# Moving a projection's first copy from ScalarE to VectorE in a fused attention kernel

## The chip, the cores and the metric

The kernel runs on one core of a Trainium2 chip. A core has TensorE (matrix products into PSUM, an on-chip memory of eight banks of 128 x 512 float32), VectorE (DVE), ScalarE (ACT), GpSimd (POOL), and DMA queues, here mostly those of SyncE (SP). The engines run side by side and wait for each other by semaphores; each works through its own instructions in order. The metric is the device time of one execution in microseconds (us), as the median of several runs.

## The reference

The input x is 8 batches of 512 rows of 512 numbers; cond is one row of 512 per batch. Attention with 16 heads of 32 is computed in float32:

```python
Q = x @ Wq.T + bq;  K = x @ Wk.T + bk;  V = x @ Wv.T + bv      # split into heads
cQ = Q + (cond @ Wq.T + bq);  cK = K + (cond @ Wk.T + bk)
scores = einsum('bhqd,bhkd->bhqk', cQ, cK) / sqrt(32)
out = x + merge_heads(softmax(scores) @ V)
```

## The kernel before

**Tiles.** Four heads fill the 128 partitions, so there are four head groups per batch and T = 32 of them in all; t counts them. For each t the scores are computed twice. One pass has queries on the partitions: `row_max` makes the scores of 128 queries for four heads (`row_scores`, L499), VectorE takes each row's maximum, negated (L490 for one bank, L508 for two at once), and `denominators` (L518) lets ScalarE compute exp(score - maximum) with a running sum; only the sum is kept. The other pass has keys on the partitions: `exponentials` puts the maxima into PSUM with four small bf16 products (L570), adds the scores (L573), and ScalarE writes their exponentials e (L584), which `weighted` multiplies by V (L589). The maxima get from one layout to the other by `split_max` (four small GpSimd operations that split each into three bf16 parts, L532 to L535) and `turn_max` (a transposing DMA, L544, in SP's queue).

**Projections.** Q, K and V of the next batch are made by a scheme of seven half-size products in place of eight (as Strassen's). `first_products` makes products 1, 6, half of 2, and 7; `other_products` makes 4, 5, the rest of 2, and 3. Each takes 14 matmuls of 256 columns (L403 for V, L406 for Q and K). In `first_products` the first product is copied out of its bank by ScalarE (L438, the result is called m1), and VectorE then makes three sums with it and the other products: c12 (L444), c1 (L445) and c22 (L429 for Q and K, L426 for V, by `plus`).

**The loop.** For t from 0 to 28 there are four stages, which are told apart below as the q, weighted, k and v stage. Each begins with `exponentials` for t (so with L570), then has `row_max` for a later quarter, and then either a projection with the denominators inside it (q, k and v stage) or the denominators and `weighted` for t - 1. At odd t the projections are `first_products`, at even t `other_products` (from t = 1 on). In the q stage a transpose of x on VectorE follows (`turn_x`, L323), in the k stage `split_max`, `turn_max` and the loads of the residual, which GpSimd adds to the bias (L173).

**Order and banks.** The order on TensorE, ScalarE, VectorE and GpSimd is the order of the program text; that of the DMAs in SP's queue is chosen by a planner. The banks are written out by hand: `TURNS` has a row of eight banks for each stage, the first four for `exponentials` and, when those have been read, for the projection, and the last four for the scores of `row_max`. Rows 4 to 7 are the four stages at odd t, rows 0 to 3 those at even t. A bank that a stage has filled last with scores is read by VectorE (maximum) and ScalarE (denominator) and is written again in the next stage:

```python
(6, 7, 4, 5, 0, 1, 2, 3),   # row 4, q stage at odd t: product 1 goes to bank 6, the scores to 0 to 3
(4, 5, 0, 1, 2, 3, 6, 7),   # row 5, weighted stage: its scores go to 2 and 3, and 6 and 7
(2, 5, 0, 1, 6, 7, 3, 4),   # row 6, k stage: product 1 in bank 2, scores in 6, 7, 3, 4
(6, 7, 0, 1, 2, 3, 4, 5),   # row 7, v stage: product 1 in bank 6, scores in 2 to 5
```

So in the weighted stage at odd t the first score takes the bank of the q stage's third denominator, the second that of the fourth, the third that of product 1 (read last by c22), the last that of c1. After the k stage the order is c22's bank, third, fourth, c1's; after the v stage third, fourth, c22's, c1's.

Of the kernel before, what the change touches and what calls it, by code (L numbers as in the profile page):

```python
# [12 lines left out]
ALU = mybir.AluOpType  # L13
AX = mybir.AxisListType
# [3 lines left out]
def kernel(  # L18
# [38 lines left out]
    nc = tc.nc  # L57
# [5 lines left out]
    HG = P // HD  # L63
# [4 lines left out]
    T = B * G  # L68
    HS = S // 2
# [42 lines left out]
    def banks(i, n=1):  # L112

        j = TURNS[turn[0]][i]
        if n == 1:
            return psum[:, j, :]
        k = TURNS[turn[0]][i + 1]
        return psum[:, j : k + 1 : k - j, :]
# [126 lines left out]
    for i in range(NS):  # L245
        r = slice(i * BL, (i + 1) * BL)
# [95 lines left out]
    def pair_of(t, n):  # L342

        if (n, t // 2) not in pairs:
            pairs[n, t // 2] = qkp.tile([P, 2, S], F32, tag=n, name=f"{n}T_{t // 2}")
        return pairs[n, t // 2]
# [50 lines left out]
    def product(n, b, u, i, pt, kcs=(0, 1)):  # L397

        for kc in kcs:
            w = block_of_w(n, i, u, kc)  # L400
            if n == "v":
                xb = block_of_x(b, i, kc, slice(u * P, (u + 1) * P))
                nc.tensor.matmul(pt, xb, w, start=(kc == kcs[0]), stop=(kc == kcs[-1]))  # L403
            else:
                xb = block_of_x(b, i, kc, slice(0, HS))
                nc.tensor.matmul(pt, w, xb, start=(kc == kcs[0]), stop=(kc == kcs[-1]))  # L406

    def twice(a):
        return a.unsqueeze(1).broadcast_to([P, 2, HS])

    def halves(a):
        return a.rearrange("p (h s) -> p h s", h=2)


    def parts_of(n, b, u):

        if n == "v":
            v = vs[b % 2]
            return v[:, u::2, :HS], v[:, u + 2, :HS], v[:, u::2, HS:], v[:, u + 2, HS:]
        o = pair_of(b * G + u * 2, n)  # L420
        return halves(o[:, 0, :]), o[:, 0, HS:], halves(o[:, 1, :]), o[:, 1, HS:]

    def plus(n, b, u, g, o, pt, rest):

        if n == "v":
            nc.vector.tensor_tensor(o, pt, rest, ALU.add)  # L426
        else:
            add = tok[:, "qk".index(n), u * 2 + g, b : b + 1]
            nc.vector.scalar_tensor_tensor(o, pt, add, rest, ALU.add, ALU.add)  # L429

    def first_products(n, b, u, dens, small, at, first=0):


        one_, two_ = banks(first), banks(at)
        c1, c12, c2, c22 = parts_of(n, b, u)
        m1 = c2[:, 0, :]
        product(n, b, u, 1, one_[:, :HS])
        nc.scalar.copy(m1, one_[:, :HS])  # L438
        dens()
        product(n, b, u, 6, two_[:, :HS])  # L440
        small()
        product(n, b, u, 2, two_[:, HS:], (0,))
        product(n, b, u, 7, one_[:, HS:])
        nc.vector.tensor_tensor(c12, two_[:, :HS], m1, ALU.add)  # L444
        nc.vector.tensor_tensor(c1[:, 0, :], two_[:, HS:], m1, ALU.add)  # L445
        plus(n, b, u, 1, c22, one_[:, HS:], c12)

    def other_products(n, b, u, dens, small, at):

        dens()  # L450
        one_, two_ = banks(at[0]), banks(at[1])
        product(n, b, u, 4, one_[:, :HS])
        product(n, b, u, 5, one_[:, HS:])
        small()
        product(n, b, u, 2, two_[:, :HS], (1,))
        product(n, b, u, 3, two_[:, HS:])
        c1, c12, c2, c22 = parts_of(n, b, u)
        nc.vector.tensor_tensor(c12, one_[:, HS:], c12, ALU.add)
        nc.vector.tensor_tensor(c2, halves(one_), twice(c22), ALU.add)
        plus(n, b, u, 0, c1, halves(two_), c1)  # L460
        if n != "v":
            for g in range(2):
                qkT[n, b * G + u * 2 + g] = pair_of(b * G + u * 2, n)[:, g, :]

    def project_pair(n, b, r, dens, small, at):

        if b >= B:
            dens()
            small()
        else:  # L470
            (first_products, other_products)[r % 2](n, b, r // 2, dens, small, at)


    nmax = {}
    sums = {}

    def open_max(t):
        if t not in nmax:
            nmax[t] = op.tile([P, NS, HG, 1], F32, tag="nmax", name=f"nmax_{t}", bufs=3)
            sums[t] = op.tile([P, NS, HG, 1], F32, tag="sums", name=f"sums_{t}", bufs=3)  # L480

    def row_max(t, qc):
        if t >= T:
            return
        open_max(t)
        for j in range(HG):
            row_scores(t, qc, j, banks(HG + j))
        if t < T - 2 or t * NS + qc == T * NS - 1:
            for j in range(2):
                nc.vector.tensor_reduce(  # L490
                    nmax[t][:, qc, j : j + 1, 0], banks(HG + j), AX.X, ALU.max, negate=True
                )
        else:
            row_max_of(t, qc, 0, banks(HG, 2))
        row_max_of(t, qc, 1, banks(HG + 2, 2))

    def row_scores(t, qc, j, pt):
        r = slice(j * HD, (j + 1) * HD)
        nc.tensor.matmul(  # L499
            pt,  # L500
            qkT["q", t][r, qc * P : (qc + 1) * P],
            qkT["k", t][r, :],
            start=True,
            stop=True,
        )

    def row_max_of(t, qc, pr, pt):
        nc.vector.tensor_reduce(  # L508
            nmax[t][:, qc, pr * 2 : pr * 2 + 2, 0], pt, AX.X, ALU.max, negate=True
        )  # L510

    def denominators(t, qc, prs=range(NP)):

        if t >= T - 2:
            return
        for j in [pr * 2 + i for pr in prs for i in range(2)]:
            dead = op.tile([P, S], F32, tag="dead", name=f"dead_{t}_{qc}_{j}")
            nc.scalar.activation(  # L518
                dead,
                banks(HG + j),  # L520
                AF.Exp,
                bias=nmax[t][:, qc, j, :],
                accum_out=sums[t][:, qc, j, :],
            )

    def split_max(t, on=nc.gpsimd):

        if t >= T:
            return
        m, sp = nmax[t], split[t % 2]  # L530
        rest = op.tile([P, NS, HG, 1], F32, tag="rest", name=f"rest_{t}")
        on.tensor_copy(sp[:, :, :, 0:1], m)  # L532
        on.tensor_tensor(rest, m, sp[:, :, :, 0:1], ALU.subtract)
        on.tensor_copy(sp[:, :, :, 1:2], rest)
        on.tensor_tensor(sp[:, :, :, 2:3], rest, sp[:, :, :, 1:2], ALU.subtract)  # L535
# [3 lines left out]
    def turn_max(t):  # L539

        if t >= T:
            return
        maxT[t] = op.tile([P, S], BF16, tag="maxT", name=f"maxT_{t}")
        nc.sync.dma_start_transpose(  # L544
            maxT[t].rearrange("p (c q) -> p c q", c=NS),
            split[t % 2].rearrange("p c h e -> p (c h e)"),
        )
# [258 lines left out]
    for t in range(T - 3):  # L806
        b, r = divmod(t, G)

        exponentials(t, 0)
        row_max(t + 1, 1)  # L810
        of = ((t - 1) // G + 1, (t - 1) % G)
        dens = lambda: denominators(t + 1, 1)
        if t:
            project_pair("q", *of, dens, nothing, 1 if r % 2 else (0, 3))
        else:
            first_products("v", 0, 0, dens, nothing, 1)
            turn_x(NC + 2)
            load_residual(1)
        turn_x(t + NC + 3)
        advance()  # L820

        exponentials(t, 1)
        row_max(t + 1, 2)
        dens = lambda: denominators(t + 1, 2)
        if t:
            dens()
            weighted(
                t - 1, banks(0), banks(1), lambda: combine_x(b + 1, r) if r < 2 else None
            )
        else:  # L830
            dens()
            other_products("v", 0, 0, nothing, nothing, (0, 2))
        advance()

        exponentials(t, 2)
        row_max(t + 1, 3)
        split_max(t + 1)
        turn_max(t + 1)
        dens = lambda: denominators(t + 1, 3)
        if t:  # L840
            project_pair("k", *of, dens, nothing, 1 if r % 2 else (0, 3))
        else:
            first_products("v", 0, 1, dens, nothing, 1)
            combine_x(1, 0)
        if t:
            load_residual(t + 1)
        advance()

        exponentials(t, 3)
        row_max(t + 2, 0)  # L850
        dens = lambda: denominators(t + 2, 0)

        project_pair("v", *of, dens, nothing, 1 if r % 2 else (0, 2))
        advance()


# [55 lines left out]
    t = T - 3  # L912
# [21 lines left out]
    t = T - 2  # L934
# [15 lines left out]
    pa, rest = banks(2), [1, 2, 3]  # L950
# [8 lines left out]
    t = T - 1  # L959
# [47 lines left out]
    b, g = divmod(t, G)  # L1007
# [55 lines left out]
```

## Time and the profile before

| | |
|---|---|
| median of 3 runs | 722.1 us (721.99 to 722.43) |
| profiled execution | 722.59 us, of which the span from the first to the last instruction is 720.8 |
| granted TensorE clock | 0.999 |
| TensorE, ScalarE, VectorE, GpSimd busy | 99%, 86%, 73%, 24% of the span |
| L438, ScalarE copy 128x256 | 46 instructions, 402 ns at the median for Q and K, 372 for V |
| L490, maximum of one bank | 240 instructions, 686 ns |
| L508, maximum of two banks | 130 instructions, 1214 ns |

A line of the timeline has start and length in us, the engine, the line of the program, what is written from what, and in brackets how long the engine had been idle and what it waited for; several like instructions can be merged (x4). PEld is TensorE's loading of weights, which runs ahead of the products. A line of the table by stretches has the stretch, its length, and for TensorE, weight loads, VectorE, ScalarE and GpSimd the busy time and the instructions, then the granted clock, the busy share of the DMA engines and GB/s. A line of the waits has total us, times, and the longest. Ends of matmuls are modelled, so a busy TensorE can still be a waiting one.

### The profile page before, as it was taken

To read this page: it belongs to the slowest core of one execution; us is meant where nothing else is said; L and a number is where in the kernel's file an instruction comes from. 1 tells how busy PE (TensorE), PEld (TensorE's weight loads), DVE (VectorE), ACT (ScalarE), POOL (GpSimd) and SP (SyncE) were. 2 spreads that over 40 slices of the span, in tenths; PEclk is the share of its full clock that TensorE was granted. 3 is DMA by queue.
4 is the path that set the end of the run, shared out by engine and by line. 5 is a ranking of instruction groups with operands and counts; after the bars stand their busy time and mean duration, and the time that the engine had idled before them with its cause. 6 is when DMAs were issued, how large, how long until landed. Compare 5 with 4: busy or idle time off the path is not lost.

```text
span 720.8 us, 14892 instructions
## 1 busy us (share of the span) xinstructions
PE 714.2 (99%) x5296; PEld 401.3 (56%) x5296; DVE 528.0 (73%) x834; ACT 617.3 (86%) x1539; POOL 176.3 (24%) x275
## 2 busy tenths in 40 slices
PE   9999999999999999999999999999999999999997
PEld 7566555565555566555565555565555565555532
DVE  4798777777768777677776877777767767767777
ACT  2589989999899998989999889998989989889674
POOL 3712221122221122221122221122221122221351
PEclk9999999999999999999999999999999999999999
DMA  6733321222322222321322321323201222211211
GB/s 177 110 60 62 53 41 30 49 44 46 53 35 36 50 41 49 53 41 28 51 41 49 52 40 27 53 37 52 38 16 23 38 38 38 37 21 19 37 32 29
DMA packets 223358, 32.91 MB, mean 46 GB/s; under 512 B 221610, under 2 KB 222122, under 8 KB 223284
## 3 DMA queue, kind: packets, MB, share of 16 engines
q1 hardware_dynamic: 221524, 30.92, 25.3%
q10 hardware_dynamic: 1760, 1.05, 0.5%
q8 instruction: 41, 0.67, 0.4%
q14 instruction: 33, 0.27, 0.1%
HBM read 19.75 MB, written 8.39 MB: 39 GB/s over the span
## 4 chain that ended last, share of the span: by engine, by line
PE 97%; DVE 2%; issue 1%; DMA 1%; DVEq 0%
PE psum L406 27%; PE psum L499 16%; PE psum L589 15%; PE psum L403 14%; PE psum L573 14%; PE psum L570 5%; PE psum L350 2%; DVE acc L863 1%; PE psum L889 1%; DMA w_q<-in_L_cond_Wq_dram 1%; PE psum L266 0%; DVE acc L861 0%; PE psum L311 0%; PE psum L667 0%; PE psum L599 0%
## 5 line engine op out<-in xcount | busy, mean ns | idle before, releaser
L518 ACT ACTIVATE dead<-psum,nmax 128x512 f32<-128x512 f32 x480 | 327.6, 702 | 5.1 <-DVE nmax L490 3.1
L584 ACT ACTIVATE e<-psum 128x512 f32<-128x512 f32 x488 | 252.0, 602 | 64.2 <-PE psum L573 63.9
L490 DVE TENSOR_REDUCE nmax<-psum 128x1 f32<-128x512 f32 x240 | 154.5, 686 | 143.1 <-PE psum L499 143.1
L508 DVE TENSOR_REDUCE nmax<-psum 128x2 f32<-128x1024 f32 x130 | 157.7, 1214 | 2.8 <-PE psum L499 2.7
L499 PE MATMUL psum<-kT,qT 32*128 32x512 f32 x1024 | 143.9, 605 | 0.0
L646 POOL TENSOR_TENSOR res<-res,recs 128x512 f32<-128x512 f32 x30 | 31.5, 1049 | 432.1 <-DVE res L645 432.1
L573 PE MATMUL psum<-qT,kT 32*128 32x512 f32 x976 | 125.5, 587 | 0.0
L589 PE MATMUL psum<-e,v 128*32 128x512 f32 x1024 | 121.2, 596 | 0.0
L518 ACT ACTIVATION_READ_ACCUMULATOR dead<-psum,nmax 128x1 f32 x480 | 105.2, 219 | 0.0
L499 PEld LDWEIGHTS psum<-kT,qT 32*128 32x128 f32 x1024 | 59.8, 183 | 58.1 <-ACT dead L518 26.4
L589 PEld LDWEIGHTS psum<-e,v 128*32 128x32 f32 x1024 | 26.6, 110 | 65.1 <-issue 37.6
L573 PEld LDWEIGHTS psum<-qT,kT 32*128 32x128 f32 x976 | 48.6, 185 | 2.2
L403 PE MATMUL psum<-wc_v,xc 128*128 128x256 f32 x192 | 49.3, 379 | 0.0
L570 PE MATMUL psum<-maxT,onesb 3*128 3x512 bf16 x488 | 48.1, 384 | 0.0
L406 PE MATMUL psum<-xc,wc_k 128*128 128x256 f32 x180 | 46.2, 379 | 0.0
L406 PE MATMUL psum<-xc,wc_q 128*128 128x256 f32 x180 | 46.2, 379 | 0.0
L570 PEld LDWEIGHTS <-onesb 3*128 3x128 bf16 x488 | 12.3, 90 | 57.2 <-issue 57.2
L173 POOL TENSOR_TENSOR xr<-xr,bvs 128x512 f32<-128x512 f32 x31 | 39.4, 1272 | 18.7 <-DMA x<-in_x_dram 12.0
L403 PEld LDWEIGHTS psum<-wc_v,xc 128*128 128x128 f32 x192 | 36.5, 190 | 5.0
L647 POOL TENSOR_TENSOR res<-res,xr 128x512 f32<-128x512 f32 x30 | 38.2, 1273 | 2.4
L403 PE MATMUL psum<-wT_v,xT 128*128 128x256 f32 x128 | 37.1, 392 | 0.0
L406 PEld LDWEIGHTS psum<-xc,wc_k 128*128 128x128 f32 x180 | 34.2, 190 | 4.7
(165 smaller groups left out, 791.2 us busy)
## 6 DMA issues: line engine op xcount, KB each, us to landing
xr<-in_x_dram SPq DMA_DIRECT2D x124, 64.0 KB, 2.4
out_dram<-res SPq DMA_DIRECT2D x122, 64.0 KB, 1.9
x<-in_x_dram SPq DMA_DIRECT2D x112, 64.0 KB, 2.4
w_q<-in_L_cond_Wq_dram SPq DMA_DIRECT2D x4, 256.0 KB, 4.4
w_v<-in_L_cond_Wv_dram SPq DMA_DIRECT2D x16, 64.0 KB, 2.4
w_k<-in_L_cond_Wk_dram SPq DMA_DIRECT2D x16, 48.0 KB, 2.3
x<-in_x_dram ACTq DMA_DIRECT2D x2, 256.0 KB, 3.9
x<-in_x_dram SPq DMA_DIRECT2D x2, 256.0 KB, 4.2
```

The costliest lines, as they stand in the source:

```text
L173: nc.gpsimd.tensor_tensor(xr[t], xr[t], bias, ALU.add)
L403: nc.tensor.matmul(pt, xb, w, start=(kc == kcs[0]), stop=(kc == kcs[-1]))
L406: nc.tensor.matmul(pt, w, xb, start=(kc == kcs[0]), stop=(kc == kcs[-1]))
L490: nc.vector.tensor_reduce(nmax[t][:, qc, j : j + 1, 0], banks(HG + j), AX.X, ALU.max, negate=True)
L499: nc.tensor.matmul(pt, qkT["q", t][r, qc * P : (qc + 1) * P], qkT["k", t][r, :], start=True, stop=True,)
L508: nc.vector.tensor_reduce(nmax[t][:, qc, pr * 2 : pr * 2 + 2, 0], pt, AX.X, ALU.max, negate=True)
L518: nc.scalar.activation(dead, banks(HG + j), AF.Exp, bias=nmax[t][:, qc, j, :], accum_out=sums[t][:, qc, j, :],)
L570: nc.tensor.matmul(bank[j], onesb[r, :], maxT[t][r, :], start=True, stop=False)
L573: nc.tensor.matmul(bank[j], qkT["k", t][r, kc * P : (kc + 1) * P], qkT["q", t][r, :], start=False, stop=True,)
L584: nc.scalar.activation(e[:, i, :], bank[pr * 2 + i], AF.Exp)
L589: nc.tensor.matmul(pt[j * HD : (j + 1) * HD, :], vs[b % 2][:, kc, (g * HG + j) * HD : (g * HG + j + 1) * HD], es[t, kc, j // 2][:, j % 2, ...
L647: nc.gpsimd.tensor_tensor(y, y, xr.pop(t), ALU.add)
```

## The change

At odd t, in the q, k and v stages, the first product is copied by VectorE instead of ScalarE. On VectorE the copy stands between the second and the third maximum of the stage, and the last two maxima, which were one instruction over two banks, become two. To place them so, `row_max` can hand back its last two maxima as a function (`held`), which `first_products` calls behind the copy; in the k stage this function also holds `split_max` and `turn_max`. At even t, where the projection is `other_products`, they are called where they were before; so are they at t = 0, and the copies before the loop and at t = 0 stay on ScalarE.

```diff
-    def first_products(n, b, u, dens, small, at, first=0):
+    def first_products(n, b, u, dens, small, at, first=0, held=None):
...
         product(n, b, u, 1, one_[:, :HS])
-        nc.scalar.copy(m1, one_[:, :HS])
+        if held:
+            nc.vector.tensor_copy(m1, one_[:, :HS])
+            held()
+        else:
+            nc.scalar.copy(m1, one_[:, :HS])
         dens()
...
-    def project_pair(n, b, r, dens, small, at):
-
+    def project_pair(n, b, r, dens, small, at, held):
+
+        if r % 2:
+            held()
         if b >= B:
             dens()
             small()
-        else:
-            (first_products, other_products)[r % 2](n, b, r // 2, dens, small, at)
+        elif r % 2:
+            other_products(n, b, r // 2, dens, small, at)
+        else:
+            first_products(n, b, r // 2, dens, small, at, 0, held)
...
+    def one_max(t, qc, j, pt):
+        nc.vector.tensor_reduce(
+            nmax[t][:, qc, j : j + 1, 0], pt, AX.X, ALU.max, negate=True
+        )
+
-    def row_max(t, qc):
+    def row_max(t, qc, hold=False):
...
-        row_max_of(t, qc, 1, banks(HG + 2, 2))
+        last, both = [banks(HG + 2), banks(HG + 3)], banks(HG + 2, 2)
+
+        def held():
+            if hold and t < T - 2:
+                for j in range(2):
+                    one_max(t, qc, 2 + j, last[j])
+            else:
+                row_max_of(t, qc, 1, both)
+
+        if hold:
+            return held
+        held()
+        return nothing
...
         exponentials(t, 0)
-        row_max(t + 1, 1)
+        held = row_max(t + 1, 1, r % 2)
...
-            project_pair("q", *of, dens, nothing, 1 if r % 2 else (0, 3))
+            project_pair("q", *of, dens, nothing, 1 if r % 2 else (0, 3), held)
...
         exponentials(t, 2)
-        row_max(t + 1, 3)
-        split_max(t + 1)
-        turn_max(t + 1)
+        rest = row_max(t + 1, 3, r % 2)
+
+        def held():
+            rest()
+            split_max(t + 1)
+            turn_max(t + 1)
+
         dens = lambda: denominators(t + 1, 3)
         if t:
-            project_pair("k", *of, dens, nothing, 1 if r % 2 else (0, 3))
-        else:
+            project_pair("k", *of, dens, nothing, 1 if r % 2 else (0, 3), held)
+        else:
+            held()
...
         exponentials(t, 3)
-        row_max(t + 2, 0)
+        held = row_max(t + 2, 0, r % 2)
...
-        project_pair("v", *of, dens, nothing, 1 if r % 2 else (0, 2))
+        project_pair("v", *of, dens, nothing, 1 if r % 2 else (0, 2), held)
```

More of the change, by code (lines that the diff above doesn't have):

```diff
@@ L489, in row_max @@
             for j in range(2):
-                nc.vector.tensor_reduce(
-                    nmax[t][:, qc, j : j + 1, 0], banks(HG + j), AX.X, ALU.max, negate=True
-                )
+                one_max(t, qc, j, banks(HG + j))
         else:
             row_max_of(t, qc, 0, banks(HG, 2))
-        row_max_of(t, qc, 1, banks(HG + 2, 2))
+        last, both = [banks(HG + 2), banks(HG + 3)], banks(HG + 2, 2)
[9 more added lines that the diff above has]
+        return nothing
     def row_scores(t, qc, j, pt):
```

## The prediction

> **What bounds the kernel now.** I read the busy shares and the chain of waits of the page first.
>
> ```profile
> PE 714.2 (99%) x5296; PEld 401.3 (56%) x5296; DVE 528.0 (73%) x834; ACT 617.3 (86%) x1539; POOL 176.3 (24%) x275
> ...
> PE 97%; DVE 2%; issue 1%; DMA 1%; DVEq 0%
> ```
>
> TensorE is busy from end to end, and the chain names it for 97% and ScalarE not at all. Read alone, this says that relieving ScalarE is worth nothing. But a busy TensorE may be waiting between two pieces of one instruction group, so next I cut the loop into its stages (each begins with the four small L570 matmuls) and asked for the table by stretches. These are the four stages of t = 13 and the first two of t = 14; the first number is the length.
>
> ```profile
> 326.98:332.24 5.26, 5.26 (x35) 3.53 (x34) 3.61 (x6) 4.84 (x14) 0.00 (x0) 1.00 0.00 0
> 332.24:338.03 5.79, 5.79 (x62) 1.91 (x62) 5.08 (x10) 5.54 (x15) 0.00 (x0) 1.00 0.31 49
> 338.03:343.29 5.26, 5.26 (x38) 3.49 (x35) 3.90 (x7) 4.30 (x12) 2.81 (x5) 1.00 0.16 27
> 343.29:348.65 5.36, 5.36 (x35) 3.47 (x35) 3.66 (x7) 5.11 (x14) 1.96 (x4) 1.00 0.57 98
> 348.65:354.00 5.35, 5.35 (x36) 3.48 (x36) 3.70 (x7) 5.08 (x15) 0.00 (x0) 1.00 0.01 3
> 354.00:359.68 5.68, 5.68 (x62) 1.74 (x62) 4.09 (x7) 5.16 (x14) 0.00 (x0) 1.00 0.29 46
> ```
>
> The same matmuls take 5.26 us in one projection stage and 5.35 or 5.36 in another, and a weighted stage takes 5.68 at even t and 5.79 at odd t, at a granted clock of 1.00 throughout. The long ones are those that follow a first_products stage: 5.79 after q, 5.36 after k, 5.35 after v. To the nanosecond of the trace they exceed the short ones by 102, 97 and 82 ns, the same at every odd t. The waits and the timeline (start, length, then the group) say at what:
>
> ```profile
> PEld psum L499 <- ACT dead L518: 26.4, 89, 0.8
> ```
>
> ```profile
> 333.32 0.31 PEld L499 LDWEIGHTS psum<-kT,qT 32*128 32x128 f32 x7 [0.24 <-ACT dead L518]
> 333.33 1.13 PE L499 MATMUL psum<-kT,qT 32*128 32x512 f32 x8
> ```
>
> ```profile
> 354.96 0.32 PEld L499 LDWEIGHTS psum<-kT,qT 32*128 32x128 f32 x8 [0.54 <-DVE qT L429]
> ```
>
> ```profile
> 355.09 1.03 PE L499 MATMUL psum<-kT,qT 32*128 32x512 f32 x8
> ```
>
> A score's weight load waits until the last denominator exponential of the stage before (and its accumulator read) has left the bank. In the 5.79 us stage it comes at 333.32, 1.08 us after the stage began, and the scores take 1.13 us; in the 5.68 us stage at 0.96 and they take 1.03. After v it comes at 1.06 us (349.71) and costs 82 ns. So loads up to about 0.98 us are free, and each ns later costs one. Now the ScalarE row of a k stage (start 338.03), and VectorE's beside it:
>
> ```profile
> 341.24 0.40 ACT L438 COPY kT<-psum 128x256 f32<-128x256 f32 x1
> 341.51 0.71 ACT L518 ACTIVATE dead<-psum,nmax 128x512 f32<-128x512 f32 x1
> 342.09 0.22 ACT L518 ACTIVATION_READ_ACCUMULATOR dead<-psum,nmax 128x1 f32 x1
> 342.18 0.71 ACT L518 ACTIVATE dead<-psum,nmax 128x512 f32<-128x512 f32 x1
> 342.75 0.23 ACT L518 ACTIVATION_READ_ACCUMULATOR dead<-psum,nmax 128x1 f32 x1
> 342.84 0.72 ACT L518 ACTIVATE dead<-psum,nmax 128x512 f32<-128x512 f32 x1
> 343.41 0.24 ACT L518 ACTIVATION_READ_ACCUMULATOR dead<-psum,nmax 128x1 f32 x1
> 343.51 0.73 ACT L518 ACTIVATE dead<-psum,nmax 128x512 f32<-128x512 f32 x1
> 344.08 0.24 ACT L518 ACTIVATION_READ_ACCUMULATOR dead<-psum,nmax 128x1 f32 x1
> ```
>
> ```profile
> 341.37 1.22 DVE L508 TENSOR_REDUCE nmax<-psum 128x2 f32<-128x1024 f32 x1
> 342.60 0.42 DVE L444 TENSOR_TENSOR kT<-psum,kT 128x256 f32<-128x256 f32 x1
> 342.94 0.41 DVE L445 TENSOR_TENSOR kT<-psum,kT 128x256 f32<-128x256 f32 x1
> 343.40 0.48 DVE L429 SCALAR_TENSOR_TENSOR kT<-psum,tok,kT 128x256 f32<-128x256 f32 x1
> ```
>
> ScalarE runs without a gap from the copy to 344.32, which is the release that comes 1.03 us into the next stage. VectorE is idle from 343.88 to 345.50, where the next maximum waits for its scores.
>
> **The change part by part.** It acts at odd t, 1 to 27: 14 passes, three first_products stages each, 42 stages. The other four copies (before the loop and at t = 0) stay on ScalarE.
>
> *ScalarE loses the copy.* The denominators then start where the copy starts, 341.24 for 341.51, since VectorE's first maximum ended long before (340.85). At their pitch of 0.67 us the four start at 341.24, 341.91, 342.57 and 343.24, and the last read ends 0.27 us earlier, at 344.05: 0.76 us into the next stage, its load at 0.81. That is under 0.98, so the wait costs nothing any more. Gain: 14 x (102 + 97 + 82) ns = 3.93 us. More than that isn't there, since what follows is TensorE's own work: the stages with free loads take 5.26 and 5.68 us however early ScalarE is (it waits 0.96 us at the start of the k stage, which is 5.26 long).
>
> *VectorE gets the copy and splits the pair.* No VectorE copy of 128x256 out of PSUM is in the trace. Bounds: 181 ns for 128x32 (L711) and 691 ns for 128x512 (L277); on a line between them 256 columns take 420 ns, as do the 424 and 414 ns of L444 and L445 on the same shape, and I take their pitch, 0.34 us. It starts where the pair's maximum started, 341.37; its product is there by then, for ScalarE read it from 341.24. Two single maxima at the pitch of L490 (0.61 us) are 1.22 us against 1.22 for the pair, so the split itself costs nothing. The third maximum runs from 341.71 to 342.39, and the third denominator needs it at 342.57, with 0.09 us from end to start (as between a pair's end and the third denominator at even t): 0.09 us to spare. The fourth runs from 342.31 to 342.99 and is needed at 343.24. The three sums then start at 342.91 (overlapping the maximum's end by 0.09, as L458 does at even t) to 343.00, 343.25 to 343.34, and 343.58 to 343.67, and end at 344.06 to 344.16 instead of 343.88.
>
> *Who waits for the sums.* The bank that the last sum reads is written by a score of the next stage: its load comes at 0.84 to 0.94 us (end plus the 0.07 us between 343.88 and the load at 343.95), still within 0.98. Cost 0, with 0.04 to 0.14 us in hand; beyond it every ns costs one in each of 42 stages. With the upper bound for the copy (a pitch of 0.60 us, as for 512 columns) the load comes at 1.10 to 1.20 and costs 0.12 to 0.22 us x 42 = 5 to 9 us; with the lower one nothing changes. I stay near the middle, where the shape is the same.
>
> *Queued behind the copy on VectorE:* the two maxima, the three sums and, after q, the transpose of x (L323, now 333.0 to 333.7), 0.2 us later; VectorE then has 0.7 us until the next maximum at 334.38. Product 7, which writes the other half of the copied bank, starts at 4.3 us of a stage, the copy ends at 3.8.
>
> *GpSimd and the queues, k stages only.* The split of the maxima starts after the fourth maximum, 342.99 instead of 342.59, so its four instructions, the transposing DMA in SP's queue (344.07, landing in 2.6 us) and what stands behind both (the residual add L173, three x loads for it) shift by 0.40 us. The turned maxima then land at 347.1 and are first read at 348.6: 1.5 us of cover. SP's order is not written by hand, so the DMA can also come to stand behind some of the residual's loads, 0.5 us each: three of them would use the cover up. In q stages the loads of x (L151) wait for L323 in SP's queue and move 0.2 us; they fill a buffer used passes later.
>
> [...]
>
> *Sum.* The profiled execution took 722.59 us, 720.8 of span and 1.8 around it. Less 3.93 that is 718.7 (span 716.9). It stands 0.5 us above the median of the runs, so for the median I say 722.1 - 3.9 = 718.2.
>
> **The rivals.**
> Part of it taken back (0.13): one of the three kinds of stage keeps a wait, on the last sum instead of ScalarE. For it: only 0.04 us in hand at the worse end. Gain 14 x 0.18 = 2.5 us, 719.6.
> No change (0.09): the chain names no ScalarE, and the 0.1 us might belong to the stages themselves. Against it: equal matmuls, and the cost follows the load's time (1.06 and 1.08). 722.1.
> Slower (0.08): VectorE becomes the bound at the last sum. If copy and maxima take 0.24 us more than I have, the load after them comes at 1.08 us, as late as ScalarE's today: from there on it is slower, 4.2 us for each further 0.1 us. With the upper price of the copy, up to 0.22 - 0.09 = 0.13 us a stage more than now, 5 us: 727. Against it: no VectorE instruction of 256 columns takes over 0.48 us.
>
> **How the numbers follow.** The forecast has 0.70: 718.2, by itself 717.8 to 718.7 (the runs differ by 0.4). A measurement tells 0.2%, 1.4 us, from no change. Faster by that is the forecast and nearly all of the first rival, 0.81; within it the rest of that and no change, 0.11; slower 0.08. A range of 717.7 to 720.8 takes in the forecast and the first rival and leaves out less than 2 in 10.
>
> **What would show it.** Right: stages after q, k and v of odd t at 5.68, 5.26 and 5.26 us; the denominators straight behind the exponentials; the waits of L499's loads on L518 much fewer than 89, and none replaced by one on L429 that lasts beyond 0.98 us; ScalarE busy 17 us less, VectorE some 20 more. Wrong: a VectorE copy well over 0.42 us, a gap on VectorE before it, a third denominator waiting for its maximum, or L570 waiting for the turned maxima.

## The result, and the profile after

The changed kernel takes 719.4 us (median of 6 runs, 718.62 to 719.72) against 722.05 (6 runs, 721.87 to 722.67): a ratio of 0.9961, with a 95% interval of 0.9950 to 0.9972. It is faster, by 2.65 us. The profiled execution took 718.62 us, of which 716.5 is the span.

The changed kernel's lines are numbered anew: L439 is the copy, L491 the maximum of one bank, L448, L449 and L429 the three sums, L523 the scores, L542 the denominators, L594 the products of the maxima, L568 the transposing DMA. In some of the experiments they stand up to five lines further on.

The busy shares and the chain of the page:

```profile
PE 709.8 (99%) x5296; PEld 400.4 (56%) x5296; DVE 536.3 (75%) x918; ACT 604.9 (84%) x1497; POOL 176.3 (25%) x275
...
PE 95%; DVE 2%; DMA 1%; issue 1%; POOL 0%; SPq 0%; DVEq 0%; POOLq 0%
```

TensorE's share still reads 99%, although it now works 4.4 us less: what went was counted as busy. VectorE has 84 instructions more and ScalarE 42 fewer. The chain had a DMA in it before, a load of weights at the start; by line it now also names the transposing DMA (maxT<-split, 0.6%), to which I come back. The table by stretches, for the same stages as before (q, weighted, k and v stage of t = 13, q and weighted of t = 14; the first number is the length):

```profile
324.87:330.14 5.27, 5.27 (x35) 3.54 (x36) 3.98 (x9) 4.86 (x15) 0.00 (x0) 1.00 0.00 0
330.14:335.82 5.68, 5.68 (x61) 1.95 (x62) 4.91 (x10) 5.15 (x14) 0.00 (x0) 1.00 0.30 48
335.82:341.08 5.26, 5.26 (x38) 3.50 (x34) 4.02 (x9) 4.40 (x13) 2.56 (x3) 1.00 0.14 25
341.08:346.35 5.27, 5.27 (x35) 3.39 (x36) 3.81 (x9) 4.74 (x14) 2.21 (x6) 1.00 0.60 102
346.35:351.61 5.26, 5.26 (x35) 3.51 (x34) 3.87 (x8) 4.73 (x13) 0.00 (x0) 1.00 0.01 3
351.61:357.29 5.68, 5.68 (x61) 1.74 (x60) 4.12 (x7) 5.24 (x15) 0.00 (x0) 1.00 0.30 46
```

The three long stages (5.79, 5.36, 5.35) are gone: 5.68, 5.27 and 5.26. ScalarE's and VectorE's rows of the timeline, in the k stage that begins at 335.82:

```profile
339.03 0.71 ACT L542 ACTIVATE dead<-psum,nmax 128x512 f32<-128x512 f32 x1
...
341.03 0.72 ACT L542 ACTIVATE dead<-psum,nmax 128x512 f32<-128x512 f32 x1
341.60 0.24 ACT L542 ACTIVATION_READ_ACCUMULATOR dead<-psum,nmax 128x1 f32 x1
```

```profile
337.96 1.29 DVE L491 TENSOR_REDUCE nmax<-psum 128x1 f32<-128x512 f32 x2 [1.23 <-PE psum L523]
339.17 0.41 DVE L439 COPY kT<-psum 128x256 f32<-128x256 f32 x1
339.50 1.28 DVE L491 TENSOR_REDUCE nmax<-psum 128x1 f32<-128x512 f32 x2
340.69 0.41 DVE L448 TENSOR_TENSOR kT<-psum,kT 128x256 f32<-128x256 f32 x1
341.02 0.41 DVE L449 TENSOR_TENSOR kT<-psum,kT 128x256 f32<-128x256 f32 x1
341.36 0.47 DVE L429 SCALAR_TENSOR_TENSOR kT<-psum,tok,kT 128x256 f32<-128x256 f32 x1
```

ScalarE's first denominator begins 3.21 us into the stage, where its copy began before (341.24 less 338.03). The last read ends at 341.84, 0.76 us into the next stage, where it was 1.03. VectorE's last sum ends at 341.83. After the k stage the first weight load of the scores waits for that sum, as it did before (14 waits, of 3.3 us in all then and 5.5 now). The waits of such loads on the denominators have fallen from 89, of 26.4 us in all, to:

```profile
PEld psum L523 <- ACT dead L542: 17.1, 48, 0.8
```

```profile
341.88 0.48 PEld L523 LDWEIGHTS psum<-kT,qT 32*128 32x128 f32 x8 [0.37 <-DVE kT L429]
```

That load comes 0.80 us into its stage, early enough to be free: the stage takes 5.27 us.

### The profile page after: what moved, and what is told of

Same layout as the page of the kernel before. It is cut to its first block, busy times and chain, and to the rows that moved or that the text cites. A ratio compares the mean times of both kernels' runs of the same rounds, so it can differ in the third digit from the quotient of the medians.

```text
span 716.5 us, 15020 instructions
## 1 busy us (share of the span) xinstructions
PE 709.8 (99%) x5296; PEld 400.4 (56%) x5296; DVE 536.3 (75%) x918; ACT 604.9 (84%) x1497; POOL 176.3 (25%) x275
## 4 chain that ended last, share of the span: by engine, by line
PE 95%; DVE 2%; DMA 1%; issue 1%; POOL 0%; SPq 0%; DVEq 0%; POOLq 0%
PE psum L406 26%; PE psum L523 16%; PE psum L613 15%; PE psum L403 14%; PE psum L597 14%; PE psum L594 5%; PE psum L350 2%; DVE acc L891 1%; DMA x<-in_x_dram 1%; PE psum L917 1%; DMA maxT<-split 1%; DVE acc L889 0%; PE psum L691 0%; PE psum L623 0%; SPq L674 0%
## 5 line engine op out<-in xcount | busy, mean ns | idle before, releaser
L542 ACT ACTIVATE dead<-psum,nmax 128x512 f32<-128x512 f32 x480 | 327.7, 706 | 5.2 <-DVE nmax L491 3.1
L491 DVE TENSOR_REDUCE nmax<-psum 128x1 f32<-128x512 f32 x324 | 208.3, 685 | 135.6 <-PE psum L523 118.0
L523 PE MATMUL psum<-kT,qT 32*128 32x512 f32 x1024 | 140.1, 595 | 0.0
L532 DVE TENSOR_REDUCE nmax<-psum 128x2 f32<-128x1024 f32 x88 | 106.8, 1215 | 2.7 <-PE psum L523 2.7
L542 ACT ACTIVATION_READ_ACCUMULATOR dead<-psum,nmax 128x1 f32 x480 | 107.6, 224 | 0.0
L523 PEld LDWEIGHTS psum<-kT,qT 32*128 32x128 f32 x1024 | 59.7, 182 | 54.5 <-ACT dead L542 17.1
L594 PE MATMUL psum<-maxT,onesb 3*128 3x512 bf16 x488 | 48.1, 384 | 0.1
L594 PEld LDWEIGHTS <-onesb 3*128 3x128 bf16 x488 | 12.3, 90 | 57.3 <-issue 56.5
L406 PEld LDWEIGHTS psum<-xc,wc_q 128*128 128x128 f32 x180 | 34.2, 190 | 4.6
```

Of the source, the lines that this page charges most:

```text
L491: nc.vector.tensor_reduce(nmax[t][:, qc, j : j + 1, 0], pt, AX.X, ALU.max, negate=True)
L523: nc.tensor.matmul(pt, qkT["q", t][r, qc * P : (qc + 1) * P], qkT["k", t][r, :], start=True, stop=True,)
L532: nc.vector.tensor_reduce(nmax[t][:, qc, pr * 2 : pr * 2 + 2, 0], pt, AX.X, ALU.max, negate=True)
L542: nc.scalar.activation(dead, banks(HG + j), AF.Exp, bias=nmax[t][:, qc, j, :], accum_out=sums[t][:, qc, j, :],)
L594: nc.tensor.matmul(bank[j], onesb[r, :], maxT[t][r, :], start=True, stop=False)
```

## The experiments

**Why ScalarE's release is the cause: the copy given back as dead work.** VectorE does all that it does in the changed kernel, and ScalarE copies an unused buffer in the old place.

```diff
+    pad = const.tile([P, HS], F32, tag="pad", name="pad")
+    nc.vector.memset(pad, 1.0)
+    padto = const.tile([P, HS], F32, tag="padto", name="padto")
...
             nc.vector.tensor_copy(m1, one_[:, :HS])
             held()
+            nc.scalar.copy(padto, pad)
```

> VectorE has the copy and the split pair as changed, but ScalarE is given a copy of 128x256 from one buffer to another in the old place, so that its denominators start as late as before. If the gain is ScalarE's earlier release of the last bank, it is gone: 722 to 723, stages after q, k and v at odd t back at about 5.78, 5.36 and 5.35 us. If the gain came from VectorE's new order, it stays: 719.4.

Measured: 722.8 us (722.41 to 725.07, 10 runs), ratio to before 1.0011 (1.0002 to 1.0019). The stages from the q stage of t = 13 on:

```profile
326.73:332.00 5.27, 5.27 (x36) 3.55 (x36) 3.98 (x9) 4.85 (x14) 0.00 (x0) 1.00 0.00 0
332.00:337.80 5.80, 5.80 (x61) 1.91 (x61) 5.02 (x10) 5.57 (x15) 0.00 (x0) 1.00 0.31 49
337.80:343.07 5.27, 5.27 (x39) 3.51 (x36) 3.91 (x9) 4.29 (x12) 2.57 (x3) 1.00 0.15 25
343.07:348.46 5.39, 5.39 (x37) 3.50 (x37) 3.92 (x10) 5.16 (x14) 2.20 (x6) 1.00 0.58 98
348.46:353.73 5.27, 5.27 (x37) 3.48 (x37) 3.76 (x7) 4.92 (x14) 0.00 (x0) 1.00 0.01 3
```

0.4 us of ScalarE work, with nothing depending on its result, takes the gain away. The stages after q and k are even a little longer than before, by about 0.02 us, because the dead copy takes 0.43 us where the one out of PSUM took 0.40. The stage after v did not come back, though: 5.27 and not 5.35, which I had missed. Before, the real copy in the v stage began 3.31 us into it (346.60), since it had to wait for product 1, which the late loads at the stage's start had pushed back. The dead copy does not wait for product 1 and begins at 3.20 there as elsewhere (346.27). The two rows, before and with the dead copy:

```profile
346.60 0.37 ACT L438 COPY v<-psum 128x256 f32<-128x256 f32 x1
```

```profile
346.27 0.43 ACT L444 COPY padto<-pad 128x256 f32<-128x256 f32 x1
```

So the last read ends 0.93 us into the next stage and its load is still free. In the kernel before, the third wait was thus an echo of the second.

That the median comes out even a little above before's is not the waits alone. In the trace the loop is 3.86 us longer than the changed kernel's; the late loads at odd t make up about 3.4 of it, and two single stages, at t = 2 and t = 23, another 0.6. What delays those two stays open.

**The split alone.** Only the last two maxima are one by one; ScalarE keeps the copy.

```diff
-            nc.vector.tensor_copy(m1, one_[:, :HS])
             held()
+            nc.scalar.copy(m1, one_[:, :HS])
```

> Only the last two maxima one by one, at odd t; the copy stays on ScalarE. By the theory ScalarE runs without a gap from the copy to the last denominator as before, so nothing moves: 722.0, 721.6 to 722.5. If the third denominator's earlier maximum is what brings the gain: 718 to 720.

Measured: 722.37 us (722.18 to 723.1, 10 runs), ratio 1.0003 (0.9994 to 1.0013); the stages of t = 13 last 5.26, 5.78, 5.26, 5.36 and that after v 5.34. No change, as expected: an earlier maximum was worth nothing here to a ScalarE that is busy until then.

**The copy alone.** The copy is VectorE's, the last two maxima stay one instruction behind it.

```diff
-            if hold and t < T - 2:
+            if False:
                 for j in range(2):
                     one_max(t, qc, 2 + j, last[j])
```

> Only the copy moved; the last two maxima stay one instruction, now behind the copy. By the theory the pair ends 0.33 us later than before (at 4.89 us of the stage), the third denominator waits for it until 4.99, the last release comes 1.17 to 1.20 us into the next stage and its load at 1.22 to 1.25, which costs 0.24 to 0.27 us in 42 stages, 10 to 11 us over free loads: 728 to 729.5, slower than before. If the split is of no weight: 719.4.

Measured: 729.9 us (729.4 to 731.43, 4 runs), ratio 1.0111 (1.0094 to 1.0128): slower than before. It is 10.5 us over the changed kernel's 719.4, as expected (10 to 11); the range in microseconds, counted from a base of about 718, was 0.4 us too low at its upper end. In the k stage that begins at 340.60, and the v stage that begins at 345.86, ScalarE shows why:

```profile
344.48 0.70 ACT L542 ACTIVATE dead<-psum,nmax 128x512 f32<-128x512 f32 x1
345.05 0.22 ACT L542 ACTIVATION_READ_ACCUMULATOR dead<-psum,nmax 128x1 f32 x1
345.61 0.69 ACT L542 ACTIVATE dead<-psum,nmax 128x512 f32<-128x512 f32 x1 [0.33 <-DVE nmax L532]
346.19 0.19 ACT L542 ACTIVATION_READ_ACCUMULATOR dead<-psum,nmax 128x1 f32 x1
346.28 0.68 ACT L542 ACTIVATE dead<-psum,nmax 128x512 f32<-128x512 f32 x1
346.85 0.20 ACT L542 ACTIVATION_READ_ACCUMULATOR dead<-psum,nmax 128x1 f32 x1
```

```profile
345.86:351.39 5.53, 5.53 (x37) 3.63 (x37) 3.96 (x8) 4.91 (x13) 2.20 (x5) 1.00 0.56 95
```

```profile
347.11 0.19 PEld L523 LDWEIGHTS psum<-kT,qT 32*128 32x128 f32 x2
```

The third denominator waits 0.33 us for the pair, the last read ends at 347.05, 1.19 us into the next stage, the load that waits for it starts 1.24 us in, and that stage takes 5.53 us, 0.26 over the free one. After q it costs 0.26 too, and after v 0.21: 10.25 us at the 14 odd t. The loop is 10.67 us longer than the changed kernel's: beside these waits, two single v stages (t = 7 and 18) take 0.28 and 0.35 us more, and the 0.2 us of late maxima that the changed kernel has (see below) are not there. So the split, worth nothing by itself, is what the copy's move needs: one part loses 7.7 us, the other nothing, both together win.

**How much lateness VectorE has to give.** The changed kernel, with one more sum (result unused) ahead of the three sums, of 96 and of 256 columns.

```diff
+    pad = const.tile([P, HS], F32, tag="pad", name="pad")
+    nc.vector.memset(pad, 1.0)
+    padto = const.tile([P, HS], F32, tag="padto", name="padto")
...
+        if held:
+            nc.vector.tensor_tensor(padto[:, :96], pad[:, :96], pad[:, :96], ALU.add)
         nc.vector.tensor_tensor(c12, two_[:, :HS], m1, ALU.add)
```

> The changed kernel with one more VectorE sum of 96 columns (its result unused) in front of the three sums, in all 42 stages: the last sum ends 0.11 to 0.16 us later, and the load that waits for it moves from 0.80 to 0.91 to 0.96 us, still free. 719.4, 719.0 to 719.8. If VectorE's lateness is paid as it comes: 0.11 to 0.16 x 42 = 5 to 7 us more.

> The same with 256 columns: 0.28 to 0.33 us later, the load at 1.08 to 1.13 us, beyond the 0.98 that are free. 0.10 to 0.15 us x 42 = 4.2 to 6.3 us more: 723.6 to 725.7. If the free part is larger than I read it, 719.4; if there is none, 731 to 733.

Measured: 718.72 us (718.63 to 719.4) with 96 columns, and 725.29 (725.03 to 725.66, 4 runs each) with 256, ratios 0.9952 (0.9937 to 0.9966) and 1.0041 (1.0026 to 1.0056). With 96 the loop takes 624.18 us, as in the changed kernel (624.05 and 624.15); the time is 0.7 us below the 719.4 expected and 0.3 below the range. Of that, 0.3 us lies outside the span, see below, and the rest, by the estimate given there, ahead of the loop. The load that waits for the last sum, and the length of its v stage, first with 96 columns (the stage begins at 341.63):

```profile
342.60 0.32 PEld L528 LDWEIGHTS psum<-kT,qT 32*128 32x128 f32 x8 [0.54 <-DVE kT L432]
```

```profile
341.63:346.89 5.26, 5.26 (x35) 3.30 (x34) 3.96 (x10) 4.73 (x14) 2.20 (x6) 1.00 0.58 100
```

and with 256 (the stage begins at 344.44):

```profile
345.57 0.31 PEld L528 LDWEIGHTS psum<-kT,qT 32*128 32x128 f32 x8 [0.71 <-DVE kT L432]
```

```profile
344.44:349.87 5.43, 5.43 (x36) 3.30 (x36) 4.15 (x11) 4.90 (x14) 2.34 (x6) 1.00 0.60 103
```

A load at 0.97 us is free, one at 1.13 costs 0.17. With the rows of before (1.06: 0.08; 1.08: 0.10), the dead copy (1.10: 0.12 to 0.13) and the pair kept (1.24: 0.26) the points lie within 0.02 us of one line: nothing up to about 0.98, then one for one. It is the same here whether ScalarE (1.24: 0.26) or VectorE (1.13: 0.17) is the late one. The larger sum pushed the next instruction back by 0.33 us, the upper end of what I had given it.

**Where the rest of the forecast gain went.** The profiled execution gained 3.97 us (722.59 to 718.62), where 3.93 were forecast, the medians 2.65. That the first comes so close is partly luck: 3.69 us of it are the loop, 0.62 a loop that began earlier, and 0.3 were lost outside the span (the table below). To see what is missing I ran the changed kernel again, the changed kernel with SP's queue in program order inside the loop, and the kernel before with that order.

```diff
+    with tc.manual_schedule(engines={mybir.EngineType.SP}):
+        for t in range(T - 3):
...
```

> The changed kernel once more, beside the next two on the same chip, to see why its median gained 2.65 us where its profiled execution gained the forecast 3.9. If late transposed maxima are the reason, this trace shows the first products of some passes (L594) waiting for them by 0.1 to 1 us in all, and the loop's stages after first products otherwise at 5.68, 5.26 and 5.26 us; median 719.4. If the reason lies before the loop, the stages add up as in the first trace and the first L594 starts later than at 45.2 us.

> The changed kernel, with SP's queue in program order inside the loop: the transposing DMA stands ahead of the residual's loads (it now stands behind two of the four at odd t), and the loads follow it. If late maxima cost the missing 1.2 us, they no longer wait for loads: 718.2, 717.9 to 718.6. If they cost nothing, 719.4 as without it. If GpSimd, which now waits for its loads in order, holds something up, over 720.

> The kernel before with the same order of SP's queue. Its maxima land 1.5 us or more ahead of their use, so by the theory of late maxima nothing is gained: 722.0, 721.6 to 722.4. If the order helps by itself (less crowded transfers), 721 or less, and the gain of the order in the changed kernel is then not the change's own loss.

Measured:

| | median us (lowest to highest) | ratio to before | first L570 or L594, us | loop, us | outside the span, us |
|---|---|---|---|---|---|
| before, profiled | 722.59 | | 45.80 | 627.74 | 1.8 |
| changed, profiled | 718.62 | | 45.18 | 624.05 | 2.1 |
| changed, again | 719.33 (718.85 to 719.38, 5 runs) | 0.9956 (0.9945 to 0.9968) | 45.79 | 624.15 | 2.1 |
| changed, SP in order | 718.53 (718.22 to 718.91, 5 runs) | 0.9948 (0.9937 to 0.9960) | 45.53 | 623.87 | 1.8 |
| before, SP in order | 722.47 (722.09 to 722.88, 12 runs) | 1.0003 (0.9994 to 1.0011) | 45.36 | 627.52 | 2.1 |

The loop is the stretch from the first product of the maxima at t = 0 to the start of the stage behind t = 28. It gained 3.6 to 3.7 us, and 3.87 with SP in order (3.65 against before in the same order), against 3.93 forecast. What SP's order is worth is seen in the changed kernel: the planner now puts two of the residual's loads ahead of the transposing DMA at odd t, where one stood before. At t = 3, SP's queue and then the load behind it:

```profile
125.82 1.03 SPq L165 DMA_DIRECT2D xr<-in_x_dram  x2
126.95 1.19 SPq L568 DMA_TRANSPOSE maxT<-split  x1
128.19 2.18 SPq L165 DMA_DIRECT2D xr<-in_x_dram  x2
```

```profile
131.07 0.10 PEld L594 LDWEIGHTS <-onesb 3*128 3x128 bf16 x4 [0.47 <-DMA maxT<-split]
```

The transfer took 4.1 us to land there, not the usual 2.5, and the first load of the next stage waited for it; the v stage that ends with this wait took 5.41 us for 5.26. The waits name it twice in the first trace (0.8 us in all) and three times in the second (1.2). The other place in the first trace, t = 11, had a transfer of the usual 2.5 us, but it was issued 2.75 us into its stage and not at 1.3: the four stores of results ahead of it in the queue took 3.40 us to issue, where they took 2.08 at t = 13. With SP in order none is named, with landings of up to 4.3 us among them, and the loop is 0.2 to 0.3 us shorter. In the kernel before the same order takes 0.2 us off the loop and nothing off the median. That 0.2 is of another kind: no stage of before waits for the maxima in either order, but each of its 42 long stages is 3 to 6 ns shorter, and the changed kernel no longer has those waits.

The rest is outside the loop. One part is the time outside the span: 1.8 us in every run of before, 2.1 in every run of the changed kernel, 0.3 us that no trace shows. The other is the start. The first products wait for the first inputs to land (the one that takes w_q idled 0.43 us for it in the trace of before, 0.24 in the first one of the changed kernel), and the loop began 45.18 to 45.80 us into the span over all traces taken, and differently in two profiles of one kernel (45.18 and 45.79 for the changed one). Most runs have no trace, so what follows is an estimate: from the spans of all runs (median 720.3 before, 717.2 changed) and the remainder of the traces (675.0 and 671.4), if that is the same in every run, the loop of the typical run began at 45.3 us before and at 45.8 after, so half a us of the gain was lost ahead of the loop. By the same estimate the other seven kernels began at 45.4 to 45.7 us, the two of them that leave the copy on ScalarE at 45.6. Whether the changed program loses this, or it is a few runs' chance, stays open. Together: 3.6 less 0.3 less 0.5 is 2.8, for the 2.65 of the medians.

The changed kernel with SP in order has the lowest median of all, 718.53 us. It falls in the range that I had given for the case that late maxima cost the missing 1.2 us, but not for that reason: of its 0.8 us over the changed kernel, 0.2 to 0.3 are in the loop; the other 0.5 lie before the loop and outside the span.

## Why the prediction was right, and where it was off

**The bound.** Right. The weight loads of the next stage's scores were late, by the last release of a denominator's bank; that is shown by the dead copy, which brings the time back with no dependency on it. The page's chain, which had no ScalarE in it, was no evidence against it. One reading was too narrow: I had written that the long stages are those that follow a first_products stage. The v stage at even t follows an other_products stage and is long too, here at t = 14, before and after:

```profile
364.94:370.29 5.35, 5.35 (x35) 3.33 (x34) 4.01 (x7) 4.82 (x13) 1.95 (x4) 1.00 0.52 89
```

```profile
362.56:367.91 5.35, 5.35 (x35) 3.33 (x36) 4.01 (x7) 4.81 (x13) 1.96 (x4) 1.00 0.58 100
```

```profile
362.72 0.75 DVE L429 SCALAR_TENSOR_TENSOR kT<-psum,tok,kT 128x512 f32<-128x512 f32 x1
```

```profile
363.59 0.34 PEld L523 LDWEIGHTS psum<-kT,qT 32*128 32x128 f32 x8 [0.60 <-ACT dead L542]
```

The loads come 1.03 us or more into the stage. The row names ScalarE, whose last read had ended 0.84 us in; VectorE's last sum of the k stage, of 512 columns here, ends at 0.91, so by the rows it is the likelier one, though no run tests that. At 14 such stages this leaves 1.2 us that the change does not touch.

**ScalarE loses the copy.** Right to 0.01 us: the denominators start at 3.21 us of a stage and end 0.27 us earlier. The forecast lengths 5.68, 5.26 and 5.26 came at nearly every odd t, and the loop's 3.69 us are the 3.93 less 0.2, nearly all of it late maxima.

**The copy on VectorE.** The line between 128x32 and 128x512 gave 420 ns; it takes 415, at a pitch of 0.33. The upper bound, for which I had kept 5 to 9 us, was far off.

**The split costs nothing.** Right as a price (two maxima from 339.50 to the next start at 340.69 are 1.19 us, the pair 1.22), and as a necessity more than I said: I had checked that the third denominator finds its maximum, with 0.09 us to spare (measured: ready at 4.36 us, started at 4.55), but had not worked out what the unsplit pair would cost ScalarE, which needs the first half early: 10.25 us at the 42 stages (in all 729.9 us against 719.4).

**Who waits for the sums.** The load comes at 0.80 us (forecast 0.84 to 0.94); the free part ends between 0.97 and 1.06 (I had said 0.98). For the rival that VectorE becomes the bound, 0.17 us more work on it are not yet enough, and with 0.33 more it happens: 725.3 us.

**GpSimd and the queues.** The step where I costed nothing and something came. The maxima moved by 0.40 us as forecast, the planner put another 0.5 us load ahead of the DMA, which I had named as possible, and 1.5 us of cover were enough at nearly every t but not where the transfer took 4.1 us or the queue was held up. Cost: 0.2 to 0.3 us.

**The sum.** The term that was mis-sized is the conversion from the profiled execution to the median. I took 1.8 us outside the span and an equal start for both kernels. The first was 2.1, and the start of a single profile lies anywhere in a range of 0.6 us. So 718.2 became 719.4: the gain was two thirds of the forecast in the medians, and nine tenths in the stretch that the change touches. By the time alone that would be the first rival, one kind of stage keeping its wait (719.6); the stages rule it out, since all three kinds are at their free lengths. That the stated range holds 719.4 at all is owed to the room left for that rival, and so partly to luck.

**The busy shares.** Wrong as stated: ScalarE is busy 12 us less, not 17, VectorE 8 more, not 20. I had multiplied durations, but neighbours overlap by 0.08 to 0.13 us (a maximum of 0.69 us is followed after 0.61, ScalarE's copy of 0.40 after 0.27), so the pitch is what counts, and VectorE's last sum had been waiting: it began 0.46 us after the sum before it (342.94 and 343.40), and now follows after 0.34.

## What to carry to other kernels

Where the busiest engine reads 99% and the chain names nothing else, compare stages with the same instructions: here 0.08 to 0.10 us between equal stages, in 42 of them, was a wait of 3.93 us in all that busy time hid, and the time at which the late load came (1.06 to 1.08 us, where 0.97 was free) said what it cost. The moved copy was priced by where it stands in the order: it fits only if the pair behind it is split (719.4 us against 729.9), since its first half is needed 0.67 us before its second. And what was moved in front of the transposing DMA's source also moved that DMA, from 0.78 to 1.42 us into the v stage of t = 13, where the planner also put a second load, of 0.5 us, in front of it.

## What the runs showed of the hardware that I had not expected

The time outside the span went with the program: it was 1.74 to 1.86 us in every run of before, of the split alone, of both late sums and of the changed kernel with SP in order, 2.08 to 2.19 in every run of the changed kernel, of the dead copy and of before with SP in order, and 2.20 to 2.27 in those of the pair kept, with spans given to 0.1 us. It didn't follow the number of instructions (15,020 in the changed kernel; with the 43 of the dead copy or of a late sum added, 15,063, at 2.1 in the one and at 1.8 in the other). What sets it is open.
